# Cross-attention on one core: 28 places for probability tiles, one V buffer, two Wq buffers, and another order of the work

## The chip, the core and the metric

The kernel runs on one NeuronCore of one Trainium2 chip. The metric is the device time of one execution in microseconds (us). The core's engines run side by side, each through its own list of instructions in order, and wait for each other by semaphores: TensorE (PE) multiplies matrices into the eight banks of PSUM, VectorE (DVE) and ScalarE (ACT) read and write PSUM and SBUF, GpSimd (POOL) reads and writes SBUF, and the queue of SyncE (SP) issues the DMAs.

## What is computed

Two batches of 2048 tokens with 640 channels attend to a text of 77 tokens and, apart from that, to 77 image tokens of 1024 channels, in 20 heads of 32 channels each.

```python
q = split_heads(x @ Wq.T)
out_text = attend(q, text @ Wk.T,  text @ Wv.T)     # softmax(q k / sqrt(32)) v, 77 keys
out_ip   = attend(q, ip @ Wk_ip.T, ip @ Wv_ip.T)    # the same with the other 77 keys
out = (out_text + out_ip) @ Wo.T + bo + x
```

Everything is float32.

## The kernel before

The work is cut into ten *head groups* q = 0 to 9: two batches, and in each five groups of four heads (128 channels). A head group has two *sub-blocks* u = 2q and 2q + 1 of 1024 tokens each, and a sub-block has two blocks h of 512 tokens or eight *tiles* of 128 tokens. Banks 0 to 7 of PSUM are shared by all steps.

The whole run after a short start is one hand-held list of words, `SCHEDULE`. Each word emits a step's instructions, so the list fixes the order on every engine at once: an engine does its own instructions in the order of the words, and what it must wait for is found from the data. A word's tail after `@` names the banks (four digits, one for each head) and a `.d` at its end puts the step on DVE, where it is on POOL otherwise. The words are:

- `q.u.h`: PE makes the queries of a block (10 records in the profile, line L194); `cq.u.h`: ACT scales and copies them out (L204).
- `k.c.t`, `v.c.t`: PE projects keys and values (L133) from weights that `LK.n` loads; `ck`, `cv`: ACT copies them. `SQ.c`: DVE transposes V in squares; `VW.q` writes a head group's squares to DRAM and `VS.q` loads them back spread out.
- `Rs.u`: PE makes the scores of group s of sub-block u (L226), four heads side by side in the array, one head to each of four banks. `Ks.u`: four copies by ACT into the places for probabilities `pb` (L238). `Ms.u`: maxima by DVE (L251). `Ss.u`: subtraction (L265). `Es.u`: exponential by ACT (L272). `Ds.u`: sums by DVE (L297). `Is.u`: reciprocals by DVE (L304). `Ns.u`: normalising (L309). `Ts.u`: DVE's transposes, in place (L316).
- `A.q`: PE multiplies all 16 transposed tiles of a head group with V (160 records, L325) into four banks, `CA.q`: ACT takes the result out (L348 or L352).
- `m`, `cm`, `o`, `co`, `G`, `W`: the output projection of batch 0, in seven products (Strassen's scheme), each added by DVE to the residual (L508, L512). `o` and `p` are the last chunk of channels. It is spread over the time in which batch 1 attends.
- `V`, `X`, `F`, `Y`, `z`, `yz`: the output projection of batch 1 after A.9, with sums of weights (`V`) and of tokens (`X`), 33 products for each half (`F`, L848) and additions by DVE (`Y`, L796).
- DMAs by SP: `LX.u.h` loads a block of x for batch 1, `LQ.q` a head group's Wq, `LO` all of Wo, `LF`/`fe` fetch residuals, `st` stores results, `LW` and `LA` load for the last projection.

A group of scores is three or two tiles of one sub-block. `pb` has 24 tiles in three zones of eight: one for the second sub-block of every head group, and two by turns for the first, so that the first sub-block of head group q + 1 can be scored while A.q has not yet read head group q. V has two buffers and Wq three.

Of the kernel before, what the change touches and what calls it, by code (L numbers as in the profile page):

```python
# [9 lines left out]
F32 = mybir.dt.float32  # L10
# [10 lines left out]
def kernel(  # L21
# [26 lines left out]
    P = 128  # L48
# [9 lines left out]
    GROUPS = ((0, 3), (3, 3), (6, 2))  # L58
# [31 lines left out]
    pb = const.tile([P, SUB + 1, NT, G, LP], F32, name="pb")  # L90
    nc.gpsimd.memset(pb[:, :, :, :, 2 * L :].rearrange("p z n g l -> p (z n g) l"), 0.0)
# [99 lines left out]
    def queries(u, h, pq):  # L191
        q = step_of(u)[0]
        for k in range(NC):
            nc.tensor.matmul(  # L194
                pq,
                wqs[q % 3][:, k, :],
                xs[place_of(u, h)][:, k, :],
                start=(k == 0),
                stop=(k == NC - 1),
            )  # L200
# [18 lines left out]
    def scores(u, s, ps):  # L219

        _, b, c, _ = step_of(u)
        first, n = GROUPS[s]
        for t in range(n):
            h, st = divmod(first + t, TB // P)
            for g in range(G):
                nc.tensor.matmul(  # L226
                    ps[g][:, ts(t, 2 * L)],
                    qTs[(u, h)][g * D : (g + 1) * D, ts(st, P)],
# [18 lines left out]
    def maxima(u, s, ps=None):  # L247
        n = GROUPS[s][1] * G
# [14 lines left out]
    def subtract(u, s, eng):  # L263
        n = GROUPS[s][1] * G
# [4 lines left out]
    def exponential(u, s, ps):  # L269
# [4 lines left out]
        n = GROUPS[s][1]  # L274
# [19 lines left out]
    def sums(u, s):  # L294
        n = GROUPS[s][1] * G
# [5 lines left out]
    def invert(u, s):  # L301
        n = GROUPS[s][1] * G
# [4 lines left out]
    def normalise(u, s, eng):  # L307
        n = GROUPS[s][1] * G
# [9 lines left out]
    def attend(q, pa):  # L318

        zones = pb[:, ds(q % 2, SUB)].rearrange("p z n g (k s) -> p (z n) g k s", k=NK)  # L320
        for k in range(NK):
            for r in range(G):
                rows = slice(r * D, (r + 1) * D)
                for g in range(G):
                    nc.tensor.matmul(  # L325
                        pa[r][g * D : (g + 1) * D, :],
                        v4s[q % 2][rows, g, k, :],
# [14 lines left out]
    def take_attention(q, pa):  # L342
        b, c = divmod(q, NC)
        rows = rows_of_attention(b, c).rearrange("p i (n r s) -> p r i n s", n=NT // NH, r=G)
        for r in range(G):
# [5 lines left out]
            for sub in range(SUB):  # L351
                nc.scalar.copy(rows[:, r, ts(sub, NH)], tokens[:, ts(1 - sub, NH)])  # L352
# [50 lines left out]
    pb_flat = pb.rearrange("p z n g l -> p (z n g l)")  # L403
    pb_tiles = pb_flat.rearrange("p (n t) -> p n t", t=TB)
# [140 lines left out]
    for t in range(2):  # L545
# [345 lines left out]
```

## Time and profile before

| | |
|---|---|
| median of 3 runs (lowest, highest) | 497.81 us (497.8, 498.23) |
| the profiled execution's own time | 498.71 us |
| its span, first to last instruction | 496.9 us |
| granted TensorE clock in it | 1.00 |
| busy: PE, PE weight loads | 490.1, 288.3 us |
| busy: DVE, ACT, POOL | 441.1, 241.8, 403.7 us |
| A.9 begins, the last products begin | 427.06, 432.92 us |

Times of single instructions are starts from the beginning of the span. "Busy" is the union of an engine's recorded instructions; the ends of matmuls are modelled, so that two pipelined matmuls overlap in it, and the distance from start to start tells more than the duration. Each matmul is recorded twice. A row of the groups has its count behind `x`, then busy us, mean ns of one, and after the last bar the idle time ahead of them and what ended it. A row of a timeline has start, length, engine, line, operation, tiles and count, and in brackets the idle time ahead. A row of the chain of waits has start, length, and who.

### The profile page before, as it was taken

The numbers are of one execution on the slowest core, as the hardware profiler recorded it, in microseconds if no ns is written. First come the engines' busy times: TensorE is split into PE (matmuls) and PEld (weight loads), VectorE is DVE, ScalarE is ACT, GpSimd is POOL, SyncE is SP. The second block draws the span as 40 slices with busy tenths as digits, with TensorE's granted clock in tenths as the row PEclk, the third lists the DMA queues.
The fourth block names the chain that finished last, engine by engine and source line by source line (L and its number), as shares of the span: only waits on it lengthen the run. The fifth ranks groups of instructions, "written<-read, shape, count | busy, mean of one in ns | idle before, by whom it ended". The sixth has DMA issues, their size and how long they took to land.

```text
span 496.9 us, 9747 instructions
## 1 busy us (share of the span) xinstructions
PE 490.1 (99%) x4114; PEld 288.3 (58%) x4114; DVE 441.1 (89%) x404; ACT 241.8 (49%) x423; POOL 403.7 (81%) x173
## 2 busy tenths in 40 slices
PE   8999999999999999999999999999999999999997
PEld 5658547648647556456655655744766475444442
DVE  0078999999989989998999999799899999999886
ACT  1177557757747568567516635545764443100000
POOL 0079969999989999997995899799599999378770
PEclk9999999999999999999999999999999999999999
DMA  8990543520843835615677079345616012510026
GB/s 258 355 245 12 148 107 84 155 71 22 223 133 80 252 107 162 227 19 154 232 232 247 22 237 319 88 152 176 198 50 175 3 45 64 170 57 29 0 105 233
DMA packets 66988, 70.15 MB, mean 141 GB/s; under 512 B 3712, under 2 KB 46720, under 8 KB 66944
## 3 DMA queue, kind: packets, MB, share of 16 engines
q1 hardware_dynamic: 66224, 68.81, 44.5%
q8 instruction: 32, 0.52, 0.4%
q10 hardware_dynamic: 720, 0.72, 0.4%
q14 instruction: 12, 0.10, 0.1%
HBM read 58.21 MB, written 11.30 MB: 140 GB/s over the span
## 4 chain that ended last, share of the span: by engine, by line
PE 89%; DVE 6%; DMA 3%; SPq 1%; ACT 1%; issue 0%; DVEq 0%
PE bank L194 33%; PE bank L848 11%; PE bank L325 11%; PE bank L226 10%; PE bank L133 9%; PE bank L483 9%; PE bank L464 4%; PE bank L493 2%; DVE pb L316 2%; DMA aT<-in_L_xattn_Wk_ip_dram 2%; DMA wq<-in_L_xattn_Wq_dram 2%; DVE den L297 1%; DVE mx L251 1%; SPq L525 1%; DVE acc L508 0%; DVE acc L512 0%
## 5 line engine op out<-in xcount | busy, mean ns | idle before, releaser
L265 POOL TENSOR_TENSOR pb<-pb,mx 128x1848 f32<-128x1848 f32 (+1 forms) x55 | 162.8, 2980 | 36.0 <-DVE mx L251 35.8
L309 POOL TENSOR_TENSOR pb<-pb,rden 128x1848 f32<-128x1848 f32 (+1 forms) x59 | 172.2, 2940 | 24.0 <-DVE rden L304 21.3
L194 PE MATMUL bank<-x,wq 128*128 128x512 f32 x400 | 179.0, 599 | 0.4 <-DMA wq<-in_L_xattn_Wq_dram 0.2
L251 DVE TENSOR_REDUCE mx<-pb 128x24 f32<-128x1848 f32 (+1 forms) x60 | 109.3, 1841 | 32.2 <-ACT pb L238 32.1
L194 PEld LDWEIGHTS bank<-x,wq 128*128 128x128 f32 x400 | 74.5, 191 | 88.8 <-issue 81.2
L238 ACT COPY pb<-bank 128x462 f32<-128x462 f32 (+1 forms) x240 | 102.0, 537 | 44.5 <-PE bank L226 43.9
L272 ACT ACTIVATE pb<-pb 128x1848 f32<-128x1848 f32 (+1 forms) x60 | 94.2, 1583 | 54.7 <-POOL pb L265 53.9
L297 DVE TENSOR_REDUCE den<-pb 128x24 f32<-128x1848 f32 (+1 forms) x60 | 110.0, 1839 | 5.9 <-ACT pb L272 5.7
L316 DVE STREAM_TRANSPOSE pb<-pb 128x1920 f32<-128x1920 f32 (+1 forms) x60 | 113.9, 1923 | 0.9 <-POOL pb L309 0.8
L226 PEld LDWEIGHTS bank<-kT,qT 32*128 32x128 f32 x1280 | 45.9, 184 | 23.6 <-issue 14.2
L226 PE MATMUL bank<-kT,qT 32*128 32x154 f32 x1280 | 56.5, 305 | 1.0 <-ACT pb L238 0.7
L325 PE MATMUL bank<-pb,v 32*32 32x512 f32 x1600 | 55.2, 597 | 0.1
L204 ACT ACTIVATE qT<-bank 128x512 f32<-128x512 f32 x40 | 23.6, 597 | 52.7 <-PE bank L194 52.7
L133 PE MATMUL bank<-wo_ct,aT 128*128 128x154 f32 x320 | 45.8, 296 | 0.3 <-DMA aT<-in_L_xattn_Wk_ip_dram 0.3
L133 PEld LDWEIGHTS bank<-wo_ct,aT 128*128 128x128 f32 x320 | 43.0, 188 | 4.1 <-issue 2.7
L325 PEld LDWEIGHTS bank<-pb,v 32*32 32x32 f32 x1600 | 29.1, 103 | 23.2 <-issue 11.8
L464 PE MATMUL bank<-aT,wo_ct 128*128 128x512 f32 x80 | 36.3, 596 | 0.0
L483 PE MATMUL bank<-aT,wo_ct 128*128 128x256 f32 x128 | 32.8, 389 | 0.0
L796 DVE TENSOR_TENSOR x<-x,bank 128x512 f32<-128x512 f32 x36 | 23.6, 683 | 5.2 <-PE bank L848 4.6
L483 PEld LDWEIGHTS bank<-aT,wo_ct 128*128 128x128 f32 x128 | 23.3, 190 | 6.4 <-issue 3.7
L464 PEld LDWEIGHTS bank<-aT,wo_ct 128*128 128x128 f32 x80 | 15.0, 190 | 17.3 <-issue 17.1
L848 PE MATMUL bank<-pb 128*128 128x512 f32 x48 | 22.1, 593 | 0.0
(74 smaller groups left out, 348.0 us busy)
## 6 DMA issues: line engine op xcount, KB each, us to landing
x<-in_x_dram SPq DMA_DIRECT2D x20, 1280.0 KB, 6.9
out_dram<-acc SPq DMA_DIRECT2D x20, 256.0 KB, 2.6
x<-in_x_dram SPq DMA_DIRECT2D x18, 256.0 KB, 5.6
acc<-in_x_dram SPq DMA_DIRECT2D x16, 256.0 KB, 4.1
out_dram<-x SPq DMA_DIRECT2D x15, 256.0 KB, 2.0
v<-scr SPq DMA_DIRECT2D x40, 80.0 KB, 4.0
wq<-in_L_xattn_Wq_dram SPq DMA_DIRECT2D x9, 320.0 KB, 5.0
aT<-in_L_xattn_Wk_dram SPq DMA_DIRECT2D x5, 512.0 KB, 7.1
```

Source lines behind the costliest of these rows:

```text
L133: nc.tensor.matmul(keys_in(out), loaded[n][:, k, :], cT[:, k, :, t, :], start=(k == 0), stop=(k == NCC - 1))
L194: nc.tensor.matmul(pq, wqs[q % 3][:, k, :], xs[place_of(u, h)][:, k, :], start=(k == 0), stop=(k == NC - 1),)
L226: nc.tensor.matmul(ps[g][:, ts(t, 2 * L)], qTs[(u, h)][g * D : (g + 1) * D, ts(st, P)], kT[g * D : (g + 1) * D, c, b].rearrange("p t l -> ...
L238: nc.scalar.copy(keys_of(u, s)[:, :, g], ps[g][:, : n * 2 * L].rearrange("p (n l) -> p n l", n=n))
L251: nc.vector.tensor_reduce(mx, rows_of(u, s), AX.X, ALU.max, negate=by_rows(u, s))
L265: eng.tensor_tensor(rows_of(u, s), rows_of(u, s), maxs[(u, s)].unsqueeze(3).to_broadcast([P, n, 2, L]), ALU.subtract)
L272: nc.scalar.activation(e, e, AF.Exp)
L297: nc.vector.tensor_reduce(dens[(u, s)], rows_of(u, s), AX.X, ALU.add)
L309: eng.tensor_tensor(rows_of(u, s), rows_of(u, s), rdens[(u, s)].unsqueeze(3).to_broadcast([P, n, 2, L]), ALU.mult)
L316: nc.vector.transpose(p, p)
L325: nc.tensor.matmul(pa[r][g * D : (g + 1) * D, :], v4s[q % 2][rows, g, k, :], zones[rows, :, g, k, :], start=(k == 0), stop=(k == NK - 1),)
L483: nc.tensor.matmul(part, w_of[m][:, kp, op], t_of(m, b, i)[:, kp], start=(op == kp == 0 and m in (1, 2, 5)), stop=(op == 1 and kp == 1 and ...
```

## The change

`pb` gets 28 tiles in one row. A head group with an even number has its 16 tiles at places 0 to 15. One with an odd number has its first twelve at places 16 to 27 and its last four at 12 to 15. So twelve tiles of the next head group have places of their own beside the sixteen that an attention still has to read, where it was eight, and a group of scores may lie over the bound of the two sub-blocks: the even sub-block's third group takes the first tile of the odd one along, whose groups are then of 3, 2 and 2 tiles.

The room for this comes from the second buffer of V, the third of Wq, and the four squares of V, `vS`, which move behind the text in the room of Wo. So `VS.q` writes where A.(q - 1) reads, `LQ.q` where the queries of q - 2 read, and `LO` writes over the squares that `VW.8` and `VW.9` have to send off first.

```diff
-    GROUPS = ((0, 3), (3, 3), (6, 2))
+    GROUPS = ((0, 3), (3, 3), (6, 3)), ((1, 3), (4, 2), (6, 2))
+    EARLY = NT + NT // NH
...
-    wqs = [const.tile([P, NC, P], F32, name=f"wq_{n}") for n in range(3)]
+    wqs = [const.tile([P, NC, P], F32, name=f"wq_{n}") for n in range(2)]
...
-    v4s = [const.tile([P, G, NK, D], F32, name=f"v4_{n}") for n in range(2)]
+    v4 = const.tile([P, G, NK, D], F32, name="v4")
...
-    pb = const.tile([P, SUB + 1, NT, G, LP], F32, name="pb")
+    pb = const.tile([P, SUB * NT + EARLY, G, LP], F32, name="pb")
...
-    vS = [const.tile([P, LP], F32, name=f"vS_{n}") for n in range(4)]
...
+    vS = [wo_ct[:, ds(NCC * B * LT + n * LP, LP)] for n in range(4)]
...
+    def group(u, s):
+        return GROUPS[step_of(u)[3]][s]
+
     def pb_of(u, s):
         q, _, _, sub = step_of(u)
-        first, n = GROUPS[s]
-        return pb[:, 1 if sub else q % 2 * 2, first : first + n]
+        first, n = group(u, s)
+        tile_of_q = sub * NT + first
+        place = tile_of_q + SUB * NT if q % 2 and tile_of_q < EARLY else tile_of_q
+        return pb[:, ds(place, n)]
...
         for t in range(n):
-            h, st = divmod(first + t, TB // P)
+            v = u + (first + t) // NT
+            _, b, c, _ = step_of(v)
+            h, st = divmod((first + t) % NT, TB // P)
...
-        zones = pb[:, ds(q % 2, SUB)].rearrange("p z n g (k s) -> p (z n) g k s", k=NK)
+        zones = pb[:, ds(q % 2 * EARLY, SUB * NT)].rearrange("p n g (k s) -> p n g k s", k=NK)
...
-            for sub in range(SUB):
-                nc.scalar.copy(rows[:, r, ts(sub, NH)], tokens[:, ts(1 - sub, NH)])
+            whole = EARLY // (NT // NH)
+            nc.scalar.copy(rows[:, r, whole:], tokens[:, : NHB - whole])
+            nc.scalar.copy(rows[:, r, :whole], tokens[:, NHB - whole :])
...
-    load_wq(2)
```

The list of words is another one. It holds the same words but for `LQ.2`, which was in the start, and for the engines of some steps. Subtractions on DVE are S0.10, S1.2, S0.16 (triples), S2.9, S2.12 (pairs) before and S0.0, S1.0, S0.10, S1.6 (triples), S1.15, S1.17 (pairs) after; normalising stays on DVE for N0.12. Three of the sums G on DVE are other ones. Of the sums for the last projection, eleven steps V and two X move to DVE, eight V and three X to POOL. The two lists begin so, and this is the part around the last attentions and the end:

```diff
-        "R2.0@2031 K2.0 M2.0 R0.0@6754 K0.0 S2.0 R1.0@1032 K1.0 M0.0 S0.0 q.1.0@7 E2.0 LK.4 M1.0 S1.0 q.1.1@2 "
...
+        "R0.0@5476 LK.5 K0.0 M0.0 S0.0.d R1.0@2103 K1.0 M1.0 S1.0.d q.1.0@5 cq.1.0 v.0.0@3 cv.0.0 R2.0@5047 K2.0 "
+        "M2.0 S2.0 R0.1@2361 q.1.1@5 LK.4 K0.1 M0.1 S0.1 k.1.0@7 LK.8 E1.0 D1.0 cq.1.1 ck.1.0 R2.1@5641 I1.0 "
+        "K2.1 M2.1 R1.1@0732 K1.1 E0.1 k.1.1@5 v.0.1@4 LK.7 k.2.0@2 LK.12 N1.0 E0.0 M1.1 S1.1 cv.0.1 E1.1 D0.1 "
...
+        "M1.3 R0.4@7615 M2.3 K0.4 M0.4 v.1.1@4 cv.1.1 LK.11 R0.5@3621 T0.2 N1.2 N2.2 SQ.1 K0.5 VW.1 q.4.1@4 "
...
+        "q.12.0@0 cq.12.0 N0.9 R0.11@2376 K0.11 LX.12.1 R1.10@1045 K1.10 q.12.1@2 cq.12.1 LO T0.9 N1.9 T1.9 "
+        "M0.11 W0 M1.10 LQ.7 W1 S1.10 A.4@3751 CA.4 R1.11@0642 M0.10 m1.0@3 S0.10.d K1.11 M1.11 R2.11@0751 K2.11 "
...
+        "T2.10 cq.14.0 G4.0.d N2.11 q.13.1@1 T2.11 M1.12 M0.12 S0.12 S1.12 cq.13.1 st.0.2 A.5@2405 CA.5 cm7.0 "
+        "m4.0 R2.13@5164 cm4.0 K2.13 R0.13@7530 K0.13 G5.1.d LX.14.1 LX.15.1 R1.13@1264 q.14.1@7 K1.13 E1.12 "
...
+        "cq.16.1 cq.17.0 st.2.3 R1.16@7241 K1.16 m2.3@6 M0.16 S0.16 T1.15 M1.16 R2.16@3142 K2.16 VS.7 E0.16 "
+        "q.17.1@7 cq.17.1 S1.16 T2.15 M2.16 cm2.3 D0.16 R0.17@0152 LX.18.0 E1.16 I0.16 LX.18.1 D1.16 K0.17 "
+        "A.7@6347 M0.17 R2.17@0152 S2.16 E2.16 D2.16 I2.16 N0.16 S0.17 T0.16 CA.7 K2.17 M2.17 q.18.0@6 E0.17 "
+        "R1.17@2034 st.2.1 K1.17 D0.17 M1.17 cq.18.0 N2.16 S1.17.d LX.19.0 S2.17 I0.17 N0.17 E2.17 E1.17 D2.17 "
+        "I1.16 N1.16 q.18.1@1 LX.19.1 T2.16 R0.18@4067 K0.18 M0.18 S0.18 q.19.0@3 I2.17 N2.17 cq.18.1 R1.18@0746 "
+        "cq.19.0 R2.18@2135 T0.17 D1.17 I1.17 K1.18 M1.18 N1.17 K2.18 M2.18 T1.16 m1.3@0 fe.3.4 R0.19@6724 K0.19 "
+        "S2.18 T2.17 M0.19 T1.17 E0.18 cm1.3 o.3@3 st.2.2 D0.18 E2.18 S1.18 E1.18 D1.18 fe.3.1 co.3 m5.3@4 S0.19 "
+        "E0.19 q.19.1@5 G7.3 G6.3 VS.8 I1.18 I0.18 N0.18 cm5.3 A.8@2167 CA.8 N1.18 D0.19 m3.3 cq.19.1 R1.19@2371 "
+        "m6.3 D2.18 I2.18 fe.3.2 cm3.3 K1.19 M1.19 R2.19@3426 G4.3 S1.19 K2.19 cm6.3 st.3.0 T1.18 E1.19 p.2@7 "
+        "m7.3 N2.18 M2.19 I0.19 VS.9 T0.18 LW cm7.3 p.1@4 fe.3.3 S2.19 E2.19 D1.19 I1.19 N0.19 m4.3 T2.18 D2.19 "
+        "p.0@5 cm4.3 p.3@6 I2.19 N1.19 N2.19 T0.19 T1.19 V.D.0.p V.P.0.d T2.19 A.9@0 X.A.d@1 X.L.d@3 CA.9 "
...
```

More of the change, by code (lines that the diff above doesn't have):

```diff
@@ L87 @@
     res = const.tile([P, TB], F32, name="res")
-    pb = const.tile([P, SUB + 1, NT, G, LP], F32, name="pb")
-    nc.gpsimd.memset(pb[:, :, :, :, 2 * L :].rearrange("p z n g l -> p (z n g) l"), 0.0)
+    pb = const.tile([P, SUB * NT + EARLY, G, LP], F32, name="pb")
+    nc.gpsimd.memset(pb[:, :, :, 2 * L :].rearrange("p n g l -> p (n g) l"), 0.0)
     vT = const.tile([P, B, LP], F32, name="vT")
     nc.gpsimd.memset(vT[:, :, 2 * L :], 0.0)
-    vS = [const.tile([P, LP], F32, name=f"vS_{n}") for n in range(4)]
     wo_ct = const.tile([P, NC * C], F32, name="wo_ct")
     wo = wo_ct.rearrange("p (k o) -> p k o", k=NC)
+    vS = [wo_ct[:, ds(NCC * B * LT + n * LP, LP)] for n in range(4)]
     cT = wo_ct[:, : NCC * B * LT].rearrange("p (k b t l) -> p k b t l", k=NCC, b=B, t=2)
@@ L151, in spread_v @@
             nc.sync.dma_start(
-                out=v4s[q % 2][r * D : (r + 1) * D].rearrange("p g k d -> p g (k d)"),
+                out=v4[r * D : (r + 1) * D].rearrange("p g k d -> p g (k d)"),
                 in_=scr[q].rearrange("(g d) l -> d g l", g=G),
@@ L185, in load_wq @@
         nc.sync.dma_start(
-            out=wqs[q % 3], in_=WqT[:, ts(c, P)].rearrange("(k p) o -> p k o", p=P)
+            out=wqs[q % 2], in_=WqT[:, ts(c, P)].rearrange("(k p) o -> p k o", p=P)
         )
@@ L195, in queries @@
                 pq,
-                wqs[q % 3][:, k, :],
+                wqs[q % 2][:, k, :],
                 xs[place_of(u, h)][:, k, :],
@@ L219, in scores @@
     def scores(u, s, ps):
-        _, b, c, _ = step_of(u)
-        first, n = GROUPS[s]
+        first, n = group(u, s)
         for t in range(n):
-            h, st = divmod(first + t, TB // P)
+            v = u + (first + t) // NT
+            _, b, c, _ = step_of(v)
+            h, st = divmod((first + t) % NT, TB // P)
             for g in range(G):
@@ L227, in scores @@
                     ps[g][:, ts(t, 2 * L)],
-                    qTs[(u, h)][g * D : (g + 1) * D, ts(st, P)],
+                    qTs[(v, h)][g * D : (g + 1) * D, ts(st, P)],
                     kT[g * D : (g + 1) * D, c, b].rearrange("p t l -> p (t l)"),
@@ L234, in take @@
     def take(u, s, ps):
-        n = GROUPS[s][1]
+        n = group(u, s)[1]
         for g in range(G):
@@ L247, in maxima @@
     def maxima(u, s, ps=None):
-        n = GROUPS[s][1] * G
+        n = group(u, s)[1] * G
         mx = small.tile([P, n, 2], F32, tag=f"mx{n}", name=f"mx_{u}_{s}")
@@ L263, in subtract @@
     def subtract(u, s, eng):
-        n = GROUPS[s][1] * G
+        n = group(u, s)[1] * G
         eng.tensor_tensor(
@@ L273, in exponential @@
             return
-        n = GROUPS[s][1]
+        n = group(u, s)[1]
         for g in range(G):
@@ L294, in sums @@
     def sums(u, s):
-        n = GROUPS[s][1] * G
+        n = group(u, s)[1] * G
         dens[(u, s)] = small.tile([P, n, 2], F32, tag=f"den{n}", name=f"den_{u}_{s}")
@@ L301, in invert @@
     def invert(u, s):
-        n = GROUPS[s][1] * G
+        n = group(u, s)[1] * G
         rden = small.tile([P, n, 2], F32, tag=f"rden{n}", name=f"rden_{u}_{s}")
@@ L307, in normalise @@
     def normalise(u, s, eng):
-        n = GROUPS[s][1] * G
+        n = group(u, s)[1] * G
         eng.tensor_tensor(
@@ L326, in attend @@
                         pa[r][g * D : (g + 1) * D, :],
-                        v4s[q % 2][rows, g, k, :],
+                        v4[rows, g, k, :],
                         zones[rows, :, g, k, :],
@@ L401, in block @@
         return aT[:, m : n + 1 : n - m, ts(h, HT)]
-    pb_flat = pb.rearrange("p z n g l -> p (z n g l)")
-    pb_tiles = pb_flat.rearrange("p (n t) -> p n t", t=TB)
+    pb_flat = pb.rearrange("p n g l -> p (n g l)")
+    pb_tiles = pb_flat[:, : 3 * NT * G * LP].rearrange("p (n t) -> p n t", t=TB)
     def t_of(m, b, i):
@@ L533 @@
     load_w(3)
-    load_wq(2)
     nc.sync.dma_start(out=bo_sb, in_=bo.rearrange("(c p) -> p c", p=P))
-    warm = pb[:, 0, 0].rearrange("p g l -> p (g l)")[:, :P]
+    warm = pb[:, 0].rearrange("p g l -> p (g l)")[:, :P]
     nc.vector.memset(warm, 0.0)
```

118 rows, old and new, of the table SCHEDULE are left out of this document.

## The prediction

> **What bounds the kernel now.** I read the page's busy times first, then the table by stretches of time, then the chain of waits and the timelines of TensorE (PE) and VectorE (DVE).
>
> ```profile
> PE 490.1 (99%) x4114; PEld 288.3 (58%) x4114; DVE 441.1 (89%) x404; ACT 241.8 (49%) x423; POOL 403.7 (81%) x173
> 375.00:400.00 25.00, 25.00 (x253) 14.15 (x253) 24.86 (x23) 11.24 (x18) 24.76 (x11) 1.00 0.28 81
> 400.00:425.00 25.00, 25.00 (x120) 16.18 (x119) 24.83 (x25) 8.40 (x12) 24.28 (x11) 1.00 0.20 61
> ```
>
> The columns of the last two rows are PE, weight loads, DVE, ScalarE (ACT), GpSimd (POOL). PE has no gap to speak of, but ahead of 425 us DVE has none either: 24.86 and 24.83 us of 25. So two engines bound this kernel, PE for most of the time and DVE level with it just before the last attention A.9.
>
> "PE busy" needs care, because a matmul that waits for a bank while the one ahead drains shows no idle time. The timeline and the chain give the real steps:
>
> ```profile
> 24.04 1.59 PE L226 MATMUL bank<-kT,qT 32*128 32x154 f32 x40 [0.31 <-ACT kT L550]
> 26.29 1.07 PE L226 MATMUL bank<-kT,qT 32*128 32x154 f32 x24 [0.66 <-ACT pb L238]
> 27.29 8.85 PE L194 MATMUL bank<-x,wq 128*128 128x512 f32 x20
> 36.06 1.85 PE L226 MATMUL bank<-kT,qT 32*128 32x154 f32 x48
> 37.85 2.38 PE L133 MATMUL bank<-wo_ct,aT 128*128 128x154 f32 x16
> 97.00 1.07 PE L226 MATMUL bank<-kT,qT 32*128 32x154 f32 x24
> 98.00 8.85 PE L194 MATMUL bank<-x,wq 128*128 128x512 f32 x20
> 445.20 48.15 PE bank L848 x112
> 93.03 1.74 PE bank L226 x39
> 117.71 1.52 PE bank L226 x40
> 130.21 1.74 PE bank L226 x39
> 274.80 1.77 PE bank L226 x40
> ```
>
> Every matmul is recorded twice, so a triple of score tiles is 24 records. 48 records take 37.85 - 36.06 = 1.79 us to the next start, 24 take 98.00 - 97.00 = 1.00: 0.26 us a tile and 0.21 fixed. A full 512-column record steps at 48.15 / 112 = 0.43. The 20 records from 27.29 to 36.06 take 8.77 where 8.60 are due: 0.17 more beside a run of scores. So **each separate run of scores or attention costs about 0.4 us beyond its work**, and neighbours share it.
>
> Waits for banks are what stays above that. The first three groups, eight tiles, take 27.29 - 24.04 = 3.25 where 8 x 0.26 + 0.21 = 2.31 is due: R1.0 waits 0.94 for banks that ACT still copies from R2.0. Runs of five tiles take 1.74, 1.74, 1.77 in three rows where an undisturbed one takes 1.52. Comparing start to start over the whole trace, such waits are about 3.1 us up to A.9. That is nearly all that any new order can win back on PE ahead of A.9; behind it, 112 records in 48.15 us have no gap.
>
> **The change, part by part.**
>
> *Work.* Both orders hold the same matmuls, copies, maxima, sums and transposes. A pair of sub-blocks had groups of 3, 3, 2, 3, 3, 2 tiles and gets 3, 3, 3, 3, 2, 2: four triples and two pairs in both. ACT still takes an odd head group's attention in two copies a bank, now of 1 and 3 token blocks in place of 2 and 2. Cost 0. Counting neighbours in the two lists, runs of scores or attention go from 49 to 50: **+0.4**.
>
> *Waits for banks.* I went through both orders with the steps above and the copies' durations, and listed each reuse of a bank closer than its copy.
>
> ```profile
> 23.35 0.38 SPq L123 DMA_DIRECT2D aT<-in_L_xattn_Wv_dram  x1
> 24.86 4.96 ACT L238 COPY pb<-bank 128x308 f32<-128x308 f32 x12 [0.75 <-PE bank L226]
> L238 ACT COPY pb<-bank 128x462 f32<-128x462 f32 x160 | 76.1, 586 | 30.4 <-PE bank L226 30.4
> L204 ACT ACTIVATE qT<-bank 128x512 f32<-128x512 f32 x40 | 23.6, 597 | 52.7 <-PE bank L194 52.7
> ```
>
> ACT starts at 24.86 on R2.0, whose two tiles begin at 24.04 and take 0.52: 0.3 us later. R1.0's 0.94 goes: R0.0 and R1.0 now lie on disjoint banks. New ones are: v.0.0 comes as early as 24.04 + 1.8 + 4.3 = 30.1 us (six score tiles and one query block), and its weights, issued at 23.35, land 5.3 to 7.1 us later by the rows of the next fence (0.2); A.0 wants bank 2 only 0.55 us behind q.5.0, whose copy takes 0.6 plus that 0.3 (0.3); R2.13, R0.13, R1.13 stand in a row on bank 5 and on 1, 4, 6 (0.8, copy by copy). With smaller ones I get 1.6 where the same list for the old order gave what the trace shows within some tenths, about 2.8. **-1.2**, between 0 and -2.
>
> *Places for 28 tiles, one V buffer, two Wq buffers.* Twelve tiles of the next head group, not eight, can be scored ahead of an attention, so an attention can wait longer for its transposes at no cost. In exchange the load VS.q waits for A.(q-1), and LQ.q for the group two back. SP issues in order, so what stands behind each in its queue counts.
>
> ```profile
> v<-scr SPq DMA_DIRECT2D x40, 80.0 KB, 4.0
> wq<-in_L_xattn_Wq_dram SPq DMA_DIRECT2D x9, 320.0 KB, 5.0
> aT<-in_L_xattn_Wv_dram SPq DMA_DIRECT2D x5, 512.0 KB, 5.3
> aT<-in_L_xattn_Wk_dram SPq DMA_DIRECT2D x5, 512.0 KB, 7.1
> wo_ct<-in_L_xattn_Wo_dram SPq DMA_DIRECT2D x1, 1600.0 KB, 7.0
> ```
>
> By PE's steps the shortest way from the end of an attention to the next one is over 20 us, against 4.0 to land: 0. Wq has over 20 us against 5.0: 0. LK.8 is new in being tight: released by k.1.0, wanted by k.2.0 about 6 us later, it takes 5.3 or 7.1; I take 0, at most 1.1. The squares of V move into the room of Wo, so Wo is loaded only behind VW.9 and LX.12.1. Its 7.0 us end about when POOL reaches W0 behind N1.9. I take 0; a POOL held for 2 us there would hold only scores that are 40 us from their attention.
>
> *Subtractions on DVE.* S0.0 and S1.0 move to DVE, which has nothing to do then; S1.6, S1.15, S1.17 move there too, S2.9, S1.2, S2.12, S0.16 back to POOL. DVE gets about 1 us more in all.
>
> *The stretch ahead of A.9.* This decides. In the old order DVE's last unforced start is the addition of m6.2, and A.9 begins as T2.19 ends:
>
> ```profile
> 368.36 0.69 DVE L512 TENSOR_TENSOR acc<-acc,bank 128x512 f32<-128x512 f32 x1
> 423.45 3.56 DVE L316 STREAM_TRANSPOSE pb<-pb 128x1920 f32<-128x1920 f32 x2
> 427.06 5.52 PE L325 MATMUL bank<-pb,v 32*32 32x512 f32 x160
> L251 DVE TENSOR_REDUCE mx<-pb 128x24 f32<-128x1848 f32 x40 | 81.9, 2058 | 5.1 <-ACT pb L238 5.0
> L297 DVE TENSOR_REDUCE den<-pb 128x24 f32<-128x1848 f32 x40 | 82.2, 2058 | 5.9 <-ACT pb L272 5.7
> L316 DVE STREAM_TRANSPOSE pb<-pb 128x1920 f32<-128x1920 f32 x40 | 85.5, 2146 | 0.2 <-POOL pb L309 0.2
> L251 DVE TENSOR_REDUCE mx<-pb 128x16 f32<-128x1232 f32 x20 | 28.1, 1405 | 27.1 <-ACT pb L238 27.1
> L316 DVE STREAM_TRANSPOSE pb<-pb 128x1280 f32<-128x1280 f32 x20 | 29.5, 1477 | 0.7 <-POOL pb L309 0.7
> L304 DVE RECIPROCAL rden<-den 128x24 f32<-128x24 f32 x40 | 11.6, 295 | 1.1
> L508 DVE SCALAR_TENSOR_TENSOR acc<-bank,bo_sb,acc 128x256 f32<-128x256 f32 x32 | 13.3, 459 | 1.5 <-PE bank L493 1.4
> 28.06 4.06 DVE L251 TENSOR_REDUCE mx<-pb 128x24 f32<-128x1848 f32 x2 [0.36 <-ACT pb L238]
> 242.16 1.73 PE bank L483 x8
> 106.85 5.45 PE bank L325 x148
> ```
>
> From 368.36 to 427.01 are 58.65 us. Its 54 instructions by their means (reductions of triples 2.06, of pairs 1.40; transposes 2.15 and 1.48), less 0.06 each for overlap (2 x 2.058 against 4.06), make 57.7: DVE loses 1 us there. PE's words from the end of m6.2 to A.9 make 58.1 by the steps above (a product's record 1.73 / 8 = 0.22, an attention 5.45 with its fixed 0.2); by the starts they took about 58.9, of which some 0.3 is the wait for T2.19 and 0.5 what PE loses itself. The old order is a tie.
>
> In the new order the point is M2.16, for the scores R2.16 stand late. From it to T2.19 DVE has 14 reductions of triples (28.8), 8 of pairs (11.2), 8 and 4 transposes (23.1), 12 reciprocals (about 3.3), 8 half-bank additions (3.7), and 4.5 for the other six: 74.6, less 60 x 0.06, is 71.0, and 72.0 with the same loss. It begins 2.9 us after R2.16 (0.8 scores, 0.3, 1.8 for four copies, which overlap). So T2.19 ends 74.9 us after R2.16 begins. PE needs 73.4 from there to A.9: 26 tiles 6.8, five query blocks 21.5, o and four p's 18.0, products 13.0, two attentions 10.5, nine runs 3.7. With the 0.5 that PE loses itself, A.9 waits 1.0 for T2.19, where it waited 0.3: **+0.7**, between -0.3 (no wait) and +2.
>
> *Behind A.9.* The same 66 products in the same steps. Eleven weight sums move to DVE and eight to POOL, token sums the other way round; about +0.2 us of DVE, which 48.15 us of gapless PE has room for: 0, at most 0.5.
>
> Sum: 0.4 - 1.2 + 0.7 = -0.1 on the profiled execution's 498.71 us (span 496.9, so 1.8 around it): 498.6. That execution stands 0.9 above the median of the runs, 497.81; the same step from the median gives **497.7**.
>
> **Rivals.**
>
> *Faster: DVE keeps up and PE sets A.9.* If DVE loses nothing and instructions chain more closely than 0.06 us, T2.19 is on time, and the +0.7 becomes -0.3: 497.81 + 0.4 - 1.2 - 0.3 = 496.7; with all bank waits gone, 495. For it: DVE has more room than before at A.1, A.4, A.6 and A.7. Against it: the two full rows of DVE above, and that the same sums leave DVE less room at A.3, A.5 and A.8.
>
> *Slower: DVE loses a fight with POOL in the closing stretch.* The rows:
>
> ```profile
> 196.00 1.43 DVE L265 TENSOR_TENSOR pb<-pb,mx 128x1232 f32<-128x1232 f32 x1
> 263.37 2.55 DVE L265 TENSOR_TENSOR pb<-pb,mx 128x1232 f32<-128x1232 f32 x1
> L265 POOL TENSOR_TENSOR pb<-pb,mx 128x1848 f32<-128x1848 f32 x37 | 122.9, 3332 | 8.8 <-DVE mx L251 8.7
> ```
>
> The same subtraction on DVE takes 1.43 or 2.55, so one of them lost 1.1 us, with POOL at work on a subtraction. S1.17 now stands on DVE inside the 72 us in which nothing is to spare. Each us lost there is a us on A.9; it loses what is left of POOL's instruction, up to 3.3 if POOL has just begun. From 1.0 us lost the kernel is slower by over 0.2%. With 2.2 lost: 499.9. Against it: by the order, POOL has little queued just then.
>
> The Trainium skill, page "SBUF — State Buffer", section "Who interferes with whom", says that a DVE instruction with two SBUF inputs contends with a GpSimd instruction that reads SBUF, the later one being blocked for the whole of the other. The 2.55 against 1.43 agrees with it. By that rule S1.17 loses nothing or nearly all of 3.3, not a share, and the subtractions at the start lose nothing, since POOL then idles.
>
> *Nothing:* the places are not what the order is short of, and everything cancels, 497.8.
>
> **Chances.** The forecast 0.38 (its own range 496.8 to 498.8), faster rival 0.25, slower rival 0.22, transposes late at A.3, A.5 or A.8 for other reasons 0.10 (at a similar price), nothing 0.05. About 0.2%, 1 us, is what measurement of this kernel can tell from no change. The faster rival and the lower edge of the forecast make faster by more 0.28; most of the forecast and nothing make within 0.37; the two late cases and the forecast's upper edge make slower by more 0.35. The range 496.2 to 500.2 takes in both rivals' likeliest times.
>
> **What would show it.** R0.0 to q.1.0 without the 0.66 gap; 50 runs; a run of R2.13, R0.13, R1.13 about 0.8 longer than its 2.0; DVE full from 350 to 425 and T2.19 ending just as A.9 starts, at about 427; DVE's S1.17 at 1.43. Wrong if A.9 starts with T2.19 long done, if PE waits on a DMA of V or Wq, or if gaps appear behind A.9.

## The result, and the profile after

| | before | after |
|---|---|---|
| median (lowest, highest) of 22 runs each | 498.02 us (497.45, 498.66) | 498.84 us (498.09, 499.62) |
| ratio, 95% interval | | 1.0015 (1.0009 to 1.0022) |
| profiled execution: span, granted clock | 496.9 us, 1.00 | 497.8 us, 1.00 |
| first scores, A.9, start of the last product | 24.04, 427.06, 492.31 | 23.32, 427.74, 493.23 |
| first scores to A.9 | 403.03 us | 404.42 us |
| A.9 to the last product | 65.25 us | 65.49 us |

The change costs 0.8 us, and the interval of the ratio lies above 1: 22 runs of each tell apart less than the 0.2% that I had called no change. The loss is within the range, but on the other side of the -0.1 that I forecast. Both profiled executions stand above their medians, by 0.7 and 0.8 us. Among the kernels further down, one of twelve executions of e5 took 1257.18 us, and its ratio leaves that one out.

The page after, its busy times, and two rows of the table by stretches (columns as before):

```profile
PE 489.1 (98%) x4114; PEld 287.1 (58%) x4114; DVE 440.8 (89%) x407; ACT 241.7 (49%) x423; POOL 398.4 (80%) x170
375.00:400.00 25.00, 25.00 (x246) 14.08 (x246) 24.94 (x19) 15.22 (x23) 23.76 (x8) 1.00 0.26 80
400.00:425.00 25.00, 25.00 (x189) 15.30 (x163) 24.80 (x27) 9.55 (x16) 25.00 (x12) 1.00 0.26 78
```

PE and VectorE are as full as they were. In the fifth column GpSimd has no idle time left either in the last 25 us of this stretch, 25.00 us where it was 24.28 (in the 25 us ahead it has a little more, 23.76 us where it was 24.76).

Start to start, word by word, the two traces differ at few places. The first is the start, here in PE's timeline:

```profile
23.32 1.96 PE L233 MATMUL bank<-kT,qT 32*128 32x154 f32 x48 [0.31 <-ACT kT L559]
25.21 4.56 PE L195 MATMUL bank<-x,wq 128*128 128x512 f32 x10
30.73 2.35 PE L134 MATMUL bank<-wo_ct,aT 128*128 128x154 f32 x16 [0.96 <-DMA aT<-in_L_xattn_Wv_dram]
```

The gap of 0.66 us ahead of R1.0 is gone: six tiles take 1.89 us. But v.0.0 waits for its weights. From the first scores to v.0.0 are 7.41 us here; in three other profiled executions with the same load order (e3, e5 and e6 below) they are 6.29, in a fourth (e2) 6.51. So 1.1 us of this trace is this one execution's, and what is left from the first scores to A.9 is 403.3 us, 0.3 more than before.

The second place is A.0, in the timelines of PE and ScalarE:

```profile
77.89 5.52 PE L332 MATMUL bank<-pb,v 32*32 32x512 f32 x160
83.40 1.38 ACT L245 COPY pb<-bank 128x308 f32<-128x308 f32 x4 [0.66 <-PE bank L332]
83.87 4.48 PE L134 MATMUL bank<-wo_ct,aT 128*128 128x154 f32 x32 [0.46 <-ACT pb L245]
```

The copy K1.3 starts as A.0 ends, and k.2.1, which takes a bank of R1.3, starts behind the first of the four copies. The third place is the three groups of scores in a row, where seven tiles take 270.17 - 267.16 = 3.01 us:

```profile
267.16 1.05 PE L233 MATMUL bank<-kT,qT 32*128 32x154 f32 x18
268.50 1.74 PE L233 MATMUL bank<-kT,qT 32*128 32x154 f32 x38 [0.29 <-ACT pb L245]
270.17 4.56 PE L195 MATMUL bank<-x,wq 128*128 128x512 f32 x10
```

The fourth is A.9, in the timelines of VectorE, GpSimd and PE. Ahead of it stand S1.17 of VectorE (374.44) and what GpSimd does next (376.24):

```profile
374.44 1.44 DVE L272 TENSOR_TENSOR pb<-pb,mx 128x1232 f32<-128x1232 f32 x1
376.24 6.53 POOL L316 TENSOR_TENSOR pb<-pb,rden 128x1848 f32<-128x1848 f32 x2 [2.08 <-DVE rden L311]
421.75 3.51 DVE L323 STREAM_TRANSPOSE pb<-pb 128x1920 f32<-128x1920 f32 x2
425.19 1.08 DVE L837 TENSOR_TENSOR pb<-wo_ct 128x128 f32<-128x128 f32 x1
426.19 1.50 DVE L323 STREAM_TRANSPOSE pb<-pb 128x1280 f32<-128x1280 f32 x1
418.01 7.69 POOL L316 TENSOR_TENSOR pb<-pb,rden 128x1848 f32<-128x1848 f32 x3
425.67 0.45 POOL L837 TENSOR_TENSOR pb<-wo_ct 128x128 f32<-128x128 f32 x1
427.74 5.52 PE L332 MATMUL bank<-pb,v 32*32 32x512 f32 x160 [0.61 <-DVE pb L323]
```

T2.19 ends at 427.69 and A.9 starts at 427.74, 0.77 us later than PE's own steps would have it (0.26 before). Between T1.19 and T2.19 stands the weight sum V.P.0, which takes 1.08 us; directly behind A.9 the same kind takes 0.28. GpSimd is at N2.19 and V.D.0 meanwhile. The last place is behind A.9, in the chain of waits, where the 112 records that took 48.15 us take 48.38:

```profile
445.88 48.38 PE bank L857 x112
```

### The profile page after: what moved, and what is told of

It is laid out like the page before. It is cut to its first block, busy times and chain, and to the rows that moved or that the text cites. A ratio compares the mean times of both kernels' runs of the same rounds, so it can differ in the third digit from the quotient of the medians.

```text
span 497.8 us, 9753 instructions
## 1 busy us (share of the span) xinstructions
PE 489.1 (98%) x4114; PEld 287.1 (58%) x4114; DVE 440.8 (89%) x407; ACT 241.7 (49%) x423; POOL 398.4 (80%) x170
## 4 chain that ended last, share of the span: by engine, by line
PE 88%; DMA 4%; DVE 4%; SPq 2%; ACT 1%; issue 1%; ACTq 0%
PE bank L195 32%; PE bank L857 11%; PE bank L332 11%; PE bank L233 10%; PE bank L493 9%; PE bank L134 8%; PE bank L474 4%; PE bank L503 2%; DMA x<-in_x_dram 2%; DVE pb L323 2%; DMA aT<-in_L_xattn_Wv_dram 2%; SPq L167 1%; DVE den L304 1%; SPq L535 1%; SPq L124 0%
## 5 line engine op out<-in xcount | busy, mean ns | idle before, releaser
L272 POOL TENSOR_TENSOR pb<-pb,mx 128x1848 f32<-128x1848 f32 (+1 forms) x54 | 160.2, 2980 | 52.8 <-DVE mx L258 52.7
L233 PEld LDWEIGHTS bank<-kT,qT 32*128 32x128 f32 x1280 | 44.8, 184 | 24.9 <-issue 17.9
L332 PE MATMUL bank<-pb,v 32*32 32x512 f32 x1600 | 55.3, 597 | 0.7 <-DVE pb L323 0.6
L332 PEld LDWEIGHTS bank<-pb,v 32*32 32x32 f32 x1600 | 29.5, 103 | 23.0 <-issue 11.3
```

Source lines behind the costliest of these rows:

```text
L233: nc.tensor.matmul(ps[g][:, ts(t, 2 * L)], qTs[(v, h)][g * D : (g + 1) * D, ts(st, P)], kT[g * D : (g + 1) * D, c, b].rearrange("p t l -> ...
L272: eng.tensor_tensor(rows_of(u, s), rows_of(u, s), maxs[(u, s)].unsqueeze(3).to_broadcast([P, n, 2, L]), ALU.subtract)
L332: nc.tensor.matmul(pa[r][g * D : (g + 1) * D, :], v4[rows, g, k, :], zones[rows, :, g, k, :], start=(k == 0), stop=(k == NK - 1),)
```

## The experiments

Kernels of one group ran on one chip beside the kernel before. Each row has the measured ratio to the kernel before, and from the profile the distance from the first scores to A.9 and from there to the last product (PE's starts). The last column is the sum of the two against the kernel before (468.28 us). It leaves out how late the first scores begin, which differs from execution to execution. In the edits below, `...` stands for words of the list that are left out.

| | ratio (95% interval) | to A.9 | behind | sum against before |
|---|---|---|---|---|
| before | 1 | 403.03 | 65.25 | 0 |
| after | 1.0015 (1.0009 to 1.0022) | 404.42 | 65.49 | +1.63, without the 1.12 at v.0.0 +0.51 |
| e1_wv_first | 1.0009 (1.0000 to 1.0018) | 403.22 | 65.49 | +0.43 |
| e2_v_behind | 1.0001 (0.9992 to 1.0010) | 403.09 | 65.50 | +0.31 |
| e3_r13_banks | 1.0080 (1.0066 to 1.0093) | 406.25 | 65.49 | +3.46 |
| e4_all_three | 1.0055 (1.0042 to 1.0068) | 405.82 | 65.49 | +3.03 |
| e5_k13_first | 1.0022 (1.0012 to 1.0032) | 403.62 | 65.50 | +0.84 |
| e6_one_run_more | 1.0041 (1.0029 to 1.0053) | 404.58 | 65.48 | +1.78 |
| e7_before_wq_late | 1.0000 (0.9991 to 1.0009) | 403.04 | 65.25 | +0.01 |
| e8_three_mends | 1.0007 (0.9999 to 1.0016) | 403.19 | 65.49 | +0.40 |
| e9_r13_spread | 1.0073 (1.0060 to 1.0086) | 405.79 | 65.49 | +3.00 |
| e10_k21_free | 1.0002 (0.9993 to 1.0010) | 402.75 | 65.50 | -0.03 |
| e11_old_tail | 1.0050 (1.0036 to 1.0064) | 402.80 | 67.92 | +2.44 |
| e12_s117_pool | 1.0079 (1.0065 to 1.0093) | 406.67 | 65.49 | +3.88 |
| e13_n23_early | 0.9989 (0.9980 to 0.9998) | 402.25 | 65.37 | -0.66 |
| e14_tail_sums | 0.9983 (0.9974 to 0.9992) | 402.26 | 65.27 | -0.75 |

Two theories stood at first. *Ledger*: every wait of PE is a us of the total, wherever it stands, and the change traded some waits for others. *Queue*: VectorE and GpSimd are full and set the later attentions, so PE's waits ahead of them cost nothing.

**e1: the weights of v.0.0 earlier.**

```diff
-    for _ in range(NH * NC):
+    for _ in range(NC):
         load_x()
     load_w(2)
+    for _ in range(NC):
+        load_x()
     load_w(3)
```

> The changed kernel with one edit: the DMA of the weights of v.0.0 is issued ahead of the last five slices of x instead of behind them. In the changed kernel PE waits 1.0 us for these weights (they land at 30.60, v.0.0 starts at 30.73). Ledger theory (each wait of PE ahead of A.9 is a us of the total): the wait goes, the kernel gets 1.0 us faster than the changed one, 0.2 us faster than the kernel before. Queue theory (VectorE and GpSimd are full from about 275 us on and set the end of T2.19, however early PE is): A.9 starts when it did, at most 0.3 us is left of the gain. Third reading (the start is bound by the DMAs' throughput): q.1.1 or v.0.1 waits instead, for the slices that are now behind, and nothing is gained.

v.0.0 starts 6.29 us behind the first scores, and all of the 1.1 us against the profiled execution of the changed kernel is still there at the end. But 6.29 is what three of five executions without the edit have too: it buys safety against a late transfer, on average some 0.3 us (1.12, 0.22 and three times nothing). The measured times can't tell that from nothing: the intervals of the two ratios overlap.

**e2: two weight sums behind T2.19.**

```diff
-V.D.0.p V.P.0.d T2.19 A.9@0 X.A.d@1
+T2.19 A.9@0 V.D.0.p V.P.0.d X.A.d@1
```

> The changed kernel with one edit: the two weight sums V.D.0 (GpSimd) and V.P.0 (VectorE) stand behind T2.19 instead of ahead of it. In the changed kernel V.P.0 takes 1.08 us on VectorE where others of its kind take 0.28, while GpSimd ends N2.19. If it is V.P.0, held by GpSimd, that makes T2.19 late: T2.19 starts as N2.19 ends (425.7 instead of 426.2), A.9 waits 0.25 us in place of 0.77, and the kernel is 0.5 us faster than the changed one. If VectorE's amount of work makes it late, as the prediction had it: only V.P.0's own 0.2 to 0.3 us. If GpSimd's own queue does and V.D.0 behind it is not the cause: 0.5 too, with T2.19 starting the moment N2.19 ends.

VectorE's and PE's timelines:

```profile
425.11 1.51 DVE L323 STREAM_TRANSPOSE pb<-pb 128x1280 f32<-128x1280 f32 x1 [0.49 <-POOL pb L316]
426.55 0.25 DVE L837 TENSOR_TENSOR pb<-wo_ct 128x128 f32<-128x128 f32 x1
426.68 4.92 PE L332 MATMUL bank<-pb,v 32*32 32x512 f32 x137 [0.19 <-DVE pb L323]
```

A.9 comes 0.42 us earlier against the words ahead of it, and the same 0.42 to 0.43 came back in every later kernel with this edit. V.P.0 takes 0.25 us here, with GpSimd done. VectorE now idles 0.49 us until N2.19 is done: what is left of the wait at A.9 is GpSimd's queue, not VectorE's amount of work.

**e3: other banks at R1.13, and e4: the three edits together.**

```diff
-R2.13@5164 ... R0.13@7530 ... R1.13@1264 q.14.1@7 K1.13 E1.12 cq.14.1 R0.14@0562 ... R1.14@4710
+R2.13@5164 ... R0.13@7230 ... q.14.1@5 E1.12 R1.13@1264 cq.14.1 K1.13 R0.14@7062 ... R1.14@4510
```

> The changed kernel with other banks around R2.13, R0.13, R1.13, and q.14.1 between R0.13 and R1.13, so that R1.13 does not follow on banks that ScalarE has still to copy. The number of runs of scores stays. Ledger theory: PE's 0.70 us at R1.13 go, and with them 0.7 us of the total. Queue theory: VectorE and GpSimd, full from 275 us on, set the stretch behind it, and 0 to 0.2 us are left of the gain at A.9.

> The three edits of the other kernels together. Ledger theory: 1.0 + 0.5 + 0.7 = 2.2 us faster than the changed kernel, 1.4 faster than the kernel before. Queue theory: only the part behind N2.19, 0.5 us, and a longer wait for T2.19 at A.9 (1.5 us or more where it is 0.77).

A miss. q.14.1 comes 1.0 us earlier as meant, but R0.14 now stands directly behind R1.13 and takes two of its banks (1.3 us), and m3.1 waits 1.7 us for VectorE. The loss of about 3 us reaches the end whole, and A.9's wait for T2.19 stays as it is. That speaks against the queue theory in its strong form: the stretch ahead of A.9 is full, but it begins only when PE delivers scores. e4 shows the three edits side by side: -1.12 at v.0.0, about +3 here, -0.42 at A.9.

**e5: K1.3 ahead of E1.2 on ScalarE.**

```diff
-E0.3 E0.2 E1.2 ... A.0@2037 K1.3 k.2.1@6
+E0.3 E0.2 ... A.0@2037 K1.3 E1.2 k.2.1@6
```

> The changed kernel with one edit: ScalarE copies the scores K1.3 ahead of the exponentials E1.2 instead of behind them. In the changed kernel k.2.1, behind A.0, starts 0.43 us late, for a bank that K1.3 frees. Ledger theory (each wait of PE is a us of the total, wherever it stands): k.2.1 comes 0.4 us earlier and so does the end, 0.4 us. Rival: E1.2, now 1.8 us later, makes T1.2 and A.1 late, or the gain is taken back at A.9 by VectorE: 0 or slower.

```profile
82.23 1.37 ACT L245 COPY pb<-bank 128x308 f32<-128x308 f32 x4 [2.29 <-PE bank L332]
82.70 4.48 PE L134 MATMUL bank<-wo_ct,aT 128*128 128x154 f32 x32 [0.46 <-ACT pb L245]
```

In ScalarE's and PE's timelines the copy now waits 2.29 us, for A.0 (L332) itself, and k.2.1 is exactly as late as it was. So I had the wrong place: it is not ScalarE's queue that holds K1.3. R1.3 of an odd head group has tiles 12 and 13, whose places the even group's tiles use too, and A.0 still reads them. E1.2, moved back for nothing, makes A.1 0.33 us later.

**e6: one run of scores more.**

```diff
-R2.1@5641 ... R1.1@0732 ... k.1.1@5 v.0.1@4
+R2.1@5641 ... k.1.1@0 R1.1@3725 ... v.0.1@4
```

> The changed kernel with one edit: k.1.1 (on another bank) stands between the scores R2.1 and R1.1, which followed on each other, so that there are 51 separate runs of scores or attention instead of 50. By the first term of the prediction k.1.1 to v.0.1 and the two groups of scores take 0.4 us more from start to start, and the kernel 0.4 us more. If what I took for a fixed price of a run is only the wait for ScalarE's copies behind it: less than 0.1.

From the start of R2.1 to that of k.2.0, with the same work in between, PE takes 5.61 us in the changed kernel and 5.99 here: 0.38. The prediction's 0.4 for a separate run is shown. The Trainium skill, page "TensorEngine Tiling (Array Packing)", section "Key Properties", says that a change of the tiling mode drains TensorE. It gives no price, and the 0.38 us are in keeping with it, though no run here shows the drain itself. The rest of this kernel's loss is 0.6 at q.5.0, which waits for a copy of ScalarE's, and 0.25 at A.1.

**e7: the kernel before, with Wq's third block loaded from the list.**

```diff
-    load_wq(2)
-... q.2.1@1 cq.2.1 LK.6
+... q.2.1@1 cq.2.1 LK.6 LQ.2
```

> The kernel before with one part of the change: the DMA of the third block of Wq leaves the start and is issued in the list, behind LK.6. The prediction priced that at 0. Rival: with 320 KB less in the queue behind the first loads, the first scores start earlier (they did by 0.7 us in the profiled execution of the changed kernel): up to 0.7 us faster. It also gives a second look at how much the start scatters from one execution to the next.

No difference in time (1.0000, 0.9991 to 1.0009). The first scores begin at 23.46 instead of 24.04, yet every word behind them keeps its distance within 0.06 us. So the part of the change in Wq costs nothing, and the earlier start of the changed kernel's profile, 0.72 us, is within what scatters: in nine profiled executions with one and the same load order, that of e1, the first scores begin between 22.86 and 23.60.

**e8: three mends.** e1, e2 and e5 in one.

> The changed kernel with three edits at once: the weights of v.0.0 loaded ahead of the last slices of x, K1.3 ahead of E1.2, and V.D.0 and V.P.0 behind T2.19. Ledger theory: the three gains add, 0.3 to 1.0 at the start (by how late the weights land in an execution), 0.4 at k.2.1, 0.4 at A.9: 1.1 to 1.8 us faster than the changed kernel, 0.3 to 1.0 faster than the kernel before. Rival: what PE wins early is lost at A.9, where VectorE and GpSimd are full: level with the kernel that has only the last edit, 0.1 to 0.3 us slower than before.

The rival's size, though not its reason: level with e2, 0.40 beside 0.31 in the last column. Nothing is taken back at A.9, where e2's edit brings its 0.43 as before. It is e5's edit that takes 0.32 at A.1 in place of giving 0.4 at k.2.1.

**e9: the scores around R1.13 spread further.**

```diff
-R0.13@7530 ... R1.13@1264 q.14.1@7 K1.13 E1.12 cq.14.1 R0.14@0562 ... m1.1@3 ... R1.14@4710 ... m2.1@6 ... o.1@4 ... m5.1@7
+R0.13@7230 ... q.14.1@5 E1.12 R1.13@1264 cq.14.1 K1.13 m1.1@3 R0.14@0562 ... m2.1@7 ... R1.14@4105 ... o.1@6 ... m5.1@4
```

> The changed kernel with the weights of v.0.0 loaded earlier and V.D.0, V.P.0 behind T2.19 (with these two alone: 403.0 us from the first scores to A.9, 403.03 in the kernel before), and around R1.13: q.14.1 between R0.13 and R1.13, m1.1 ahead of R0.14, m2.1 ahead of R1.14, on other banks, so that no group of scores stands within a full block of matmuls of the one whose banks it takes. One run of scores more (0.4), none of the 0.8 us that PE waits at R1.13 and R0.14. Ledger theory: 0.4 us less from the first scores to A.9. Rival (VectorE's order behind it is upset, as it was with the first try on these banks): m3.1 waits for VectorE, 1 us or more slower.

The rival. VectorE's timeline of the changed kernel, then of this one, and a row of this one's waits of PE:

```profile
272.57 3.42 DVE L258 TENSOR_REDUCE mx<-pb 128x16 f32<-128x1232 f32 x2 [1.58 <-ACT pb L245]
```

```profile
274.92 3.42 DVE L258 TENSOR_REDUCE mx<-pb 128x16 f32<-128x1232 f32 x2 [4.89 <-ACT pb L245]
PE bank L493 <- DVE acc L518: 2.5, 1, 2.5
```

With R1.13 behind q.14.1 VectorE waits 4.89 us for its copy, where it waited 1.58, and is busy without a gap from there to the addition that frees m3.1's bank. PE loses 2.7 us at m3.1 for the 0.8 it won. In this order the wait at R1.13 is what it costs to feed VectorE in time; e3 and e9 are two tries, and no other was made.

**e10: R1.3 behind A.0** (with e1 and e2).

```diff
-q.5.0@2 cq.5.0 R1.3@6514 ... A.0@2037 K1.3 k.2.1@6 k.3.0@1 ... CA.0 ... R2.3@4032 ... R0.4@7615 ... R0.5@3621
+q.5.0@2 cq.5.0 ... A.0@0374 R1.3@6512 CA.0 K1.3 k.2.1@0 k.3.0@3 ... R2.3@4762 ... R0.4@5103 ... R0.5@7625
```

> The changed kernel with the same two edits, and R1.3 behind A.0 instead of ahead of it, with k.2.1 and k.3.0 on banks of A.0. In the changed kernel R1.3 (tiles 12 and 13 of an odd head group) shares its places with tiles that A.0 still reads: its copy K1.3 cannot start before A.0 ends, and k.2.1, which takes its bank, starts 0.53 us late; moving K1.3 ahead on ScalarE left that as it was. If it is the shared places: A.0 0.8 us earlier, no gap ahead of k.2.1, 0.5 to 0.7 us less up to A.9 and in total. If it is anything else on PE's side of A.0: k.2.1 still 0.5 late.

A.0 starts 0.76 us earlier and the gap ahead of k.2.1 is gone. Here k.2.1 takes no bank of R1.3 any more, so this run alone shows only that the wait hung on K1.3; that K1.3 waited for the shared places is e5's row, where A.0 releases it. But 0.2 is lost behind A.0 and 0.44 at A.1, where VectorE's and PE's timelines say:

```profile
109.00 1.51 DVE L323 STREAM_TRANSPOSE pb<-pb 128x1280 f32<-128x1280 f32 x1 [0.52 <-POOL pb L316]
110.61 1.93 PE L332 MATMUL bank<-pb,v 32*32 32x512 f32 x46 [0.37 <-ACT vT L701]
```

The bracket of PE names the copy that ended last by the profile; T2.3, which A.1 needs, ends at 110.51 too, having waited for GpSimd's N2.3. Here the queue theory holds: a gain of PE alone is worth nothing where the next attention waits for GpSimd.

**e11: the old order behind A.9** (with e1).

```diff
-V.D.0.p V.P.0.d T2.19 A.9@0 X.A.d@1 ...
+T2.19 A.9@0 ... V.P.0.p V.D.0.d V.I.0.p V.K.0.p V.E.0.p V.F.0.d X.B.d@0 V.H.0.d ... (the old list)
```

> The changed kernel with the weights of v.0.0 loaded earlier, and everything behind A.9 in the old order (the weight sums that stood ahead of A.9 there now directly behind it). From F31.1 to the last product PE takes 59.39 us in the kernel before and 59.63 in the changed one. If the new assignment of sums costs this: 59.4 again, 0.2 us; T2.19 in time as with V.D.0 and V.P.0 behind it, 0.4: in total 0.6 less than the changed kernel. Rival: the late weight sums, six of them now behind A.9, hold the first products, 59.9 or more.

The rival again: 67.92 us. The old closing order needs its six weight sums ahead of A.9; late, they hold the first products. It says nothing on the 0.24.

**e12: S1.17 on GpSimd** (with e1 and e2).

```diff
-S1.17.d
+S1.17
```

> The changed kernel with the weights of v.0.0 loaded earlier, V.D.0, V.P.0 behind T2.19, and the subtraction S1.17 on GpSimd instead of VectorE: 2.24 us more on GpSimd, 1.44 less on VectorE, in the stretch that ends at A.9. If VectorE's amount of work sets A.9, as the prediction had it: A.9 0.3 us earlier (all that it still waits). If GpSimd's does (N2.19 ends last, and T2.19 starts as it ends): A.9 up to 2 us later, less what GpSimd idled in that stretch.

3.9 us slower (e1 and e2 together would have 402.8 to A.9), and not where I had looked. ScalarE's timeline:

```profile
377.75 2.35 ACT L279 ACTIVATE pb<-pb 128x1232 f32<-128x1232 f32 x2 [5.82 <-POOL pb L272]
```

ScalarE waits 5.82 us for GpSimd with the exponentials of these groups, and the copies that empty PE's banks stand behind them: R1.18, R2.18, m1.3 and R0.19 come later by 1.1, 1.1, 0.3 and 1.3 us. In this order GpSimd can't take the step without that; on VectorE it costs 1.44 us and no wait.

**e13: N2.3 ahead of S0.5** on top of e10, **and e14: two sums of the closing stretch earlier** on top of that.

```diff
-q.6.0@3 S0.5 M2.4 N2.3 cq.6.0
+q.6.0@3 N2.3 S0.5 M2.4 cq.6.0
```

```diff
-X.V.d@6 Y1.1.30 X.D.p@0 V.E.0.p Y1.1.20 Y6.1.20 F6.1 ... V.H.0.p ... X.K.p@7 ... V.K.0.p
+X.V.d@6 Y6.1.20 Y1.1.30 X.D.p@0 V.E.0.p Y1.1.20 F6.1 ... V.H.0.p V.K.0.p ... X.K.p@7
```

> The kernel with R1.3 behind A.0 (weights of v.0.0 earlier, V.D.0 and V.P.0 behind T2.19; 402.75 us from the first scores to A.9, 403.03 in the kernel before), and N2.3 ahead of S0.5 on GpSimd. There A.0 came 0.76 us earlier and A.1 gave 0.44 of it back: T2.3 waited 0.52 us on VectorE for N2.3, which stood behind S0.5. If GpSimd's order is what holds A.1: A.1 0.4 us earlier, 402.3 us up to A.9, and 0.4 us faster than the kernel before by 403.03 - 402.3 - 0.24. If the gain only moves on to the next attention that waits for a transpose: 402.7 again, with a longer wait at A.2 or A.9.

> The same, with two sums of the closing stretch earlier in their queues: Y6.1.20 ahead of Y1.1.30 and Y1.1.20 on VectorE (F8.1 waits for it), V.K.0 ahead of X.K on GpSimd, so that X.O, for which F11.1 waits, comes 0.4 us earlier. If these waits are the 0.24 us that PE loses behind A.9: 0.1 to 0.2 us less from A.9 to the last product (65.49 in the changed kernel, 65.25 before). If they are not: 65.49 again.

e13 came as its first theory said, e14 only in part. GpSimd's timeline and PE's, and the chain of waits, of e14:

```profile
101.85 4.46 POOL L316 TENSOR_TENSOR pb<-pb,rden 128x1232 f32<-128x1232 f32 x2
110.77 2.83 PE L332 MATMUL bank<-pb,v 32*32 32x512 f32 x72
443.86 48.16 PE bank L859 x112
```

The two normalisations stand together, A.1 comes 0.44 us earlier (87.31 us behind the first scores in place of 87.75) and the gain arrives at A.9: 402.25 and 402.26. The 112 records are back at 48.16. But of the 0.22 us won behind A.9 (65.49 to 65.27) 0.12 is there in e13 already (65.37), which changes nothing in that stretch; the two sums account for 0.10, and where the other 0.12 came from stays open. **e14 is faster than the kernel before: 497.34 us beside 498.09, ratio 0.9983 (0.9974 to 0.9992).** The changed kernel, at 1.0015, stands above that interval.

## Why the prediction was wrong

**The step that failed is the sum of the waits for banks: -1.2 was forecast, from 2.8 down to 1.6, and about -0.3 was found.** From the first scores to A.9 the changed kernel takes 403.3 us without the late weights at v.0.0, 0.27 more than before. Of that 0.4 is the run more and 0.5 is A.9, so by difference the other waits gave -0.6, and with some 0.3 for late weights on average -0.3. The largest part that was missing is k.2.1's 0.53. I had gone through each bank with the time its copy takes, but took a copy as free to start when its scores are done, and I had priced the 28 places at 0 by looking at the loads alone. K1.3 may not start then: it writes places that A.0 still reads, by the very rule of the 28 places (the last four tiles of an odd head group share theirs). In e5 ScalarE has been idle for 2.29 us when K1.3 starts, and it starts as A.0 ends; in e10, where k.2.1 no longer hangs on it, the wait is gone. With that 0.53 my count would have been about -0.7. The remaining 0.3 or so no run here accounts for.

**v.0.0's weights.** I took 0.2. It was 1.12 in the profiled execution, 0.22 in one other and nothing in three: right as a mean of five, by luck, since it scatters with the transfers of the start. A.0's wait for bank 2, forecast at 0.3, was 0.13: from R1.3's start to A.0's are 0.76 us, where pairs that nothing holds take 0.63.

**R2.13, R0.13, R1.13** were to be 0.8 longer; seven tiles are due 7 x 0.26 + 0.21 = 2.03 and took 3.01, 0.98 longer. Nearly right, and e3 and e9 did not win it back.

**The run more, +0.4.** Right: 0.38 in e6.

**A.9: +0.7 forecast, +0.5 found.** The sum over VectorE's 60 instructions came out: T2.19 ends 427.69 - 353.23 = 74.5 us after R2.16 begins, where I had 74.9. Yet the reason was a different one, so it is partly luck that the two numbers lie close. 0.42 of the 0.77 us went when V.P.0 and V.D.0 stood behind T2.19 (e2 moves both; the row that had grown is V.P.0's), and what is left waits for GpSimd's normalisation N2.19, not for VectorE's load. I had not worked out GpSimd's queue there; it was full.

**The slower rival** had the right mechanism at the wrong instruction. S1.17 took 1.44 us and lost nothing: GpSimd idled from 374.16 to 376.24, as the argument against the rival had it. Nor would a loss have had to be nothing or nearly all of 3.3 us, as I wrote. GpSimd's timeline of the kernel before, around the prediction's two subtractions at 196.00 and 263.37 us:

```profile
192.84 7.74 POOL L265 TENSOR_TENSOR pb<-pb,mx 128x1848 f32<-128x1848 f32 x2 [1.00 <-DVE mx L251]
258.07 6.55 POOL L265 TENSOR_TENSOR pb<-pb,mx 128x1848 f32<-128x1848 f32 x2
```

At 263.37 GpSimd's second subtraction had 1.25 us left, to 264.62, and VectorE lost 1.1: a share of it. At 196.00 GpSimd was at work too; there VectorE lost nothing, and GpSimd's two took 7.74 us in place of 6.55.

V.P.0, which I had put among "the other six", stood between N2.19 on GpSimd and T2.19, with two SBUF inputs, and took 1.08 us instead of 0.25. The Trainium skill, page "SBUF — State Buffer", section "Who interferes with whom", has the later of the two blocked for the whole of the other. By that V.P.0 would be held until N2.19 ends at 425.70 and be done at about 425.95, an estimate from these rows and that section. It ended at 426.27, just behind V.D.0's 426.12. So the trace agrees that V.P.0 was held, but it seems to have been held over two instructions of GpSimd's.

**Behind A.9**: 0 forecast, at most 0.5; it was 0.24. Two sums that stood late in their queues are 0.10 of it (e14); 0.12 was gone in e13 without an edit there, so its cause is open.

**The DMA edits and the buffers** cost nothing, as said: PE has no wait on V or Wq in the changed kernel, and e7 shows it for Wq.

The sum as the runs have it: 0.4 - 0.6 + 0.3 + 0.5 + 0.2 = +0.8, where +0.8 was measured. The -0.6 in it is what the other terms leave of the trace, so what the agreement tests is the trace against the times, not that term. The places themselves had little to give: before the change PE waited at two attentions, at A.9 by 0.26 us and at A.4 by about 0.16 (R1.10 takes 1.05 us to A.4's start, a triple that nothing holds 0.89).

## What to carry to other kernels

When you go through buffers for the waits that a new order makes, ask of each copy not only when its source is ready but when its destination is free: a bank stays full as long as the places it must go to are being read. Where the next attention waits for its transposes, a us that PE wins is kept only if the engine that feeds them is early too, so follow each gain to the next place where two queues meet; e10's went at A.1 to a GpSimd instruction that stood one place too late. And before a step that others wait for, look at the small instructions just ahead of it on its engine: one of a quarter of a us can take one us there.

## What was not expected of the hardware

Executions of the same load order begin their first scores up to 0.74 us apart (22.86 to 23.60 us over the nine profiles with e1's order; 23.32 to 23.94 over the five with the changed kernel's). A transfer that is just in time in one of those five is 1.1 us late in another, while from R2.0 on, the word behind it, the same words keep their distance to within 0.06 us over nearly 400 us wherever the list was not edited. Differences between single profiles should be taken from such a point on. And GpSimd's hold on a two-input VectorE instruction can cost a short one more than its own length: 0.25 us became 1.08.
